# Vision tower on one core: tokenizer with signed differences from PSUM and an earlier start of two units, and unread products in five places

## The chip, the core and the metric

The kernel runs on one core of one Trainium2 chip: a tensor engine (PE, with weight loads shown apart as PEld), a vector engine (DVE), a scalar engine (ACT), GpSimd (POOL), and SyncE (SP), whose queue issues most of the transfers. SBUF is the working memory; matrix products land in PSUM. The metric is the device time of one execution in microseconds, the median of several runs.

## The reference

A batch of 128 images of 128 x 128 goes through a tokenizer, two attention layers and two feed-forward layers, all in float32. The part that this case changes most is the tokenizer: two convolutions, each followed by a batch normalization with given statistics.

```python
def _bn(x, g, b, m, v):
    return (x - m) * (g / jnp.sqrt(v + EPS)) + b
x = _bn(_conv(X, w1, 8), g1, b1, m1, v1)     # 8x8 patches, stride 8, 64 channels: 16 x 16 places
x = _bn(_conv(x, w2, 2), g2, b2, m2, v2)     # 4x4 taps, stride 2, 256 channels: 8 x 8 places
...                                          # rearranged to 64 tokens of 256 per image
h = h + _L0_attn_ref(_layernorm(h), ...)     # relu attention
h = h + _L0_ffn_ref(_layernorm(h), ...)      # a mixture of small attentions
h = h + _L1_attn_ref(_layernorm(h), ...)     # linear attention
h = h + _L1_ffn_ref(_layernorm(h), ...)      # 8 experts, one per token, capacity 1.25
```

The last layer picks one expert for each of the 8192 tokens (argmax of a gate), numbers the tokens within their expert, runs a two-layer network of width 1024 per expert, and adds the result in the order of the tokens.

## The kernel before

One program runs the stages after each other: `tokenizer` (0 to about 174 us of the trace), `relu_attention` (to 1106), `expert_attention` (to 1936), `linear_attention` (to 2276), `route` (to 2325) and `experts` (to 2758). Inside the stages the order of the instructions on every engine is written out by hand (`tc.manual_schedule()`): each engine takes its instructions in the order of the program, and waits where a value or a buffer is not ready.

**Tokenizer.** Partitions hold 64 channels of two halves of the data. The first convolution is done row by row, 16 rows: `conv1(r)` (L123) multiplies the row's 1024 columns by a block-diagonal weight `w1bd` in two matmuls of 512 columns (L130). Each result is a PSUM tile `pa` of a pool with two buffers (`ps1`). The first half, the even places, goes through ACT with scale `s1` and offset `o1` into `ev` (L135, two copies of 64 partitions); the second half, the odd places, goes through DVE into the first third of `h` (L132). `differences(r)` (L139) fills the other two thirds of `h` with even minus odd and odd minus shifted even (L141, L142); `ev` has a column block more than needed, cleared at its edges by six memsets on POOL (L118, L119). `between` (L146) takes differences of whole rows, on POOL (L154) except for two on DVE and one on ACT.

The second convolution is a fast scheme with three products in each direction. For each of 4 row groups `m` and 4 channel blocks `ab` there is a `Unit`: `products(i)` for i = 0, 1, 2 does 12 accumulating matmuls (L177; the trace shows two passes for each) into a PSUM tile `pc` (three buffers); ACT copies one part (`y`, L189), DVE combines the others into `z` (L200, L204); `results(k)` (L210) writes the tokens to `h2`. Combinations of the weight `w` are made on the chip: a sum on POOL (L223), a change of sign on ACT (L226), and `w02`, another sum on POOL (L227).

The order before (L219 to L257): rows 0 to 4 are convolved one after another with their differences; then come the 16 units, and each of the first 11 convolves one more row ahead of its first product (row 5 with unit (0, 0), row 6 with (0, 1), and so on).

**The ends and starts of stages.** `relu_attention` ends with `old.weights()`, `old.transpose()` (PE, L544) and `old.transposed()`, and then the attention products L441. `linear_attention` starts by loading groups, computing their statistics, and transposing on PE, followed by products at L1189. `route` ranks the tokens: scans over one-hot choices, sums over partitions on PE (`pp`, L1685 and L1686), then `past` and `be` (L1736 to L1740: how many blocks lie behind the end of each expert). Then it inverts the permutation by matmuls: for 8 groups of 8 columns, DVE builds one-hot tiles `lh` (L1724) and `hv` (L1727), ACT scales `hv` by the token's number (L1732), and PE accumulates 64 matmuls of 128 x 128 by 78 into `pi` (L1734). `rin` and `rout` from it are the indices for the indirect gathers of `experts` (L1811), whose first block is normalized, transposed (L1842) and multiplied (L1854).

Of the kernel before, what the change touches and what calls it, by code (L numbers as in the profile page):

```python
# [31 lines left out]
class Ctx:  # L32
# [3 lines left out]
    def __init__(self, tc, const):  # L36
# [6 lines left out]
        self.zero = const.tile([P, 8], F32, name="zero")  # L43
        nc.vector.memset(self.zero, 0.0)

    def tables(self, const):


        self.rin = const.tile([P, NTILE], I32, name="rin")
        self.rout = const.tile([P, NTILE], I32, name="rout")  # L50
        self.bexp = const.tile([P, NBLK + 1], I32, name="bexp")
# [10 lines left out]
def tokenizer(c, x, w1, bn1, w2, bn2):  # L62
# [6 lines left out]
    with (  # L69
# [13 lines left out]


        w1bd = wp.tile([P, P], F32, name="w1bd")
        nc.vector.memset(w1bd, 0.0)
        bnv1 = wp.tile([P, 4], F32, name="bnv1")
        bnv2 = wp.tile([P, 4, 4], F32, name="bnv2")
        for k in range(2):
            nc.sync.dma_start(w1bd[k * 64 : (k + 1) * 64, k * 64 : (k + 1) * 64], w1)  # L90
            nc.sync.dma_start(bnv1[k * 64 : (k + 1) * 64, :], bn1)
        load(0, nc.scalar)
        for r in range(1, 3):
            load(r)
# [26 lines left out]
        parts = {}  # L121

        def conv1(r):  # L123

            xt = rows.pop(r)
            parts[r] = h = hp.tile([P, 12, B], F32, tag="h", name="h")
            ev = evens[r % 3]
            for k in range(2):
                pa = ps1.tile([P, 4, B], F32, tag="pa", name="pa")
                nc.tensor.matmul(pa, w1bd, xt[:, 4 * k : 4 * k + 4], start=True, stop=True)  # L130
                if k:
                    nc.vector.tensor_scalar(h[:, 0:4], pa, s1, o1, ALU.mult, ALU.add)  # L132
                else:
                    for o, i in ((ev[0:64, 0:4], slice(0, 64)), (ev[64:128, 1:5], slice(64, P))):
                        nc.scalar.activation(o, pa[i], AF.Identity, bias=o1[i], scale=s1[i])  # L135
            if r + 3 < 16:
                load(r + 3)

        def differences(r):  # L139
            h, ev = parts[r], evens[r % 3]  # L140
# [21 lines left out]
        class Unit:  # L162
# [6 lines left out]
            def products(self, i):  # L169
                m, ab = self.m, self.ab  # L170
                pc = ps2.tile([P, 4, 4, N], F32, tag="pc", name="pc")
                for j, j0 in ((1, 0), (0, 4), (2, 8)):
                    for k in range(2):
                        u = w02[:, k, j] if i == 1 else w[:, k + i, j]
                        for par in range(2):
                            r = slice(par * 64, par * 64 + 64)
                            nc.tensor.matmul(  # L177
                                pc[r, j],
                                u[:, ab * 64 : ab * 64 + 64],
                                part(m, i, k)[:, j0 : j0 + 4, r],  # L180
                                start=(k == 0),
                                stop=(k == 1),
                            )
# [5 lines left out]
                nc.scalar.activation(  # L189
                    y,  # L190
                    pc[:, 1].rearrange("p o n -> p n o"),
                    AF.Identity,
                    bias=o2[:, a] if i == 1 else 0.0,
                    scale=s2[:, a] if i == 1 else 1.0,
                )
                o = self.z[:, i].rearrange("p n (o q) -> p n o q", q=2)
                x = pc[:, 0::2].rearrange("p q o n -> p n o q")
                if i == 1:
                    for q in range(2):
                        nc.vector.scalar_tensor_tensor(  # L200
                            o[:, :, :, q], x[:, :, :, q], s2[:, a], y, ALU.mult, ALU.add
                        )
                else:
                    nc.vector.tensor_add(o, x, bcast(y, 3, 2))  # L204

            def results(self, k):

                ab = self.ab
                f = ab // 2 * 128 + (2 * self.m + k) * 16 + ab % 2 * 8
                nc.vector.scalar_tensor_tensor(  # L210
                    h2[:, :, f : f + 8],
                    self.z[:, 2 * k],
                    (s2, n2)[k][:, ab : ab + 1],
                    self.z[:, 1],
                    ALU.mult,
                    ALU.add,
                )

        with tc.manual_schedule():  # L219
            for r in range(5):  # L220
                conv1(r)
                if r == 1:
                    nc.gpsimd.tensor_add(w[:, :, 1], w[:, :, 0], w[:, :, 2])  # L223
# [36 lines left out]
def relu_attention(c, wqkv, wmlp, bmlp):  # L260
# [8 lines left out]
    with (  # L269
# [387 lines left out]
        with tc.manual_schedule():  # L657
# [426 lines left out]
def linear_attention(c, hd, hx, out, k, wqk, bqk, wv, bv, wgb):  # L1084
# [8 lines left out]
    with (  # L1093
# [543 lines left out]
def route(c, k, gfd):  # L1637
# [5 lines left out]
    with (  # L1643
# [56 lines left out]
        nc.vector.tensor_sub(first, end, nblk)  # L1700
        nc.vector.tensor_scalar_mul(first, first, float(BLK))


        nc.vector.tensor_add(cs, cs, bcast(pp[:, 0], 1, T))
        nc.vector.scalar_tensor_tensor(oh, cs, float(CAP), oh, ALU.is_le, ALU.mult)
# [14 lines left out]
        for t0 in range(0, T, T // NQ):  # L1720
# [11 lines left out]
                nc.scalar.activation(hv[:, i], hv[:, i], AF.Copy, scale=k.token[:, t])  # L1732
            for i in range(T // NQ):
                nc.tensor.matmul(pi, lh[:, i], hv[:, i], start=(t0 + i == 0), stop=(t0 + i == T - 1))  # L1734
            if t0 == 0:
                nc.vector.tensor_tensor(past, bcast(k.blk, 2, E), bcast(end, 1, NBLK), ALU.is_ge)  # L1736
                nc.vector.tensor_reduce(be[:, 0:NBLK], past, AX.X, ALU.add)
                nc.vector.tensor_scalar_min(be[:, 0:NBLK], be[:, 0:NBLK], float(E - 1))
                nc.vector.tensor_copy(be[:, NBLK : NBLK + 1], end[:, E - 1 : E])
                nc.vector.tensor_copy(c.bexp, be)  # L1740
# [9 lines left out]
def experts(c, hx, gfd, out, w1, w2, b2, routing):  # L1750
# [9 lines left out]
    with ExitStack() as nest:  # L1760
# [138 lines left out]
        with tc.manual_schedule():  # L1899
            for n in range(2):  # L1900
                blocks[n].load()
            for n in range(2):
                blocks[n].gather((False,))
            blocks[0].moments()
            blocks[0].normal()
            blocks[0].transpose()
            for n in range(2):
                blocks[n].gather((True,))
            blocks[1].moments()
            blocks[2].gather()  # L1910
            blocks[1].normal()
# [42 lines left out]
def layout(**i):  # L1954
# [9 lines left out]
    o["w1"] = i["L0_tok_w1"].reshape(64, 64)  # L1964
    o["bn1"] = np.stack([i[f"L0_tok_{k}1"] for k in "gbmv"], axis=1)
# [5 lines left out]
    o["bn2"] = bn2.reshape(4, 8, 2, 8, 2).transpose(1, 3, 0, 2, 4).reshape(64, 4, 4)  # L1971
    q, k, v = (i[f"L0_attn_W{n}"].T for n in "qkv")

    v = v.reshape(D, 32, 8).transpose(0, 2, 1).reshape(D, D)
# [45 lines left out]
```

## Time and profile before

| What | Value |
|---|---|
| runs shown | 2759.99, 2768.24, 2768.82 us; median 2768.24 |
| the profiled execution | 2759.7 us; span from the first to the last instruction 2757.9 us |
| mean granted clock of PE | 0.971 |
| busy share | PE 94%, DVE 74%, ACT 59%, POOL 59% |
| first matmul of the first convolution | 7.51 us |
| first matmul of the second convolution | 26.98 us |
| route: `pi` | 2296.84 to 2324.4 us |
| PE idle ahead of the experts' first transpose | 7.9 us |

Busy time is the time in which an engine works on an instruction; the granted clock is 1.00 or 0.50 in the rows of a stretch. A row of a group of instructions gives line, engine, operation, output and inputs, shape and count, then the busy time in all, the mean of one in ns, and the idle time of the engine before them with what ended it.

### The profile page before, as it was taken

What the parts mean: (1) busy time and instruction counts of PE and PEld (TensorE: products, weight loads), DVE (VectorE), ACT (ScalarE), POOL (GpSimd) and SP (SyncE); (2) the same over time, 40 slices, a digit from 0 to 9 for tenths busy, and PEclk for the clock granted to TensorE, in tenths of its full rate; (3) what the DMA queues carried; (4) which work ended last, traced back from release to release, by engine and by line L of the source; (5) the groups of instructions that cost most, each with busy time, mean ns of one, the idle gap of its engine ahead of it and who ended that gap; (6) DMA issues with size and microseconds to landing.
All of it is one profiled execution on the core that took longest, in us unless ns stands there. A gap on an engine that the chain in (4) does not pass through costs nothing. (4 is left out here: it accounts for less than half of the span.)

```text
span 2757.9 us, 76947 instructions
## 1 busy us (share of the span) xinstructions
PE 2602.5 (94%) x33263; PEld 1744.7 (63%) x33263; DVE 2038.5 (74%) x3024; ACT 1628.9 (59%) x3415; POOL 1633.7 (59%) x1390
## 2 busy tenths in 40 slices
PE   8989999999999998899999999999799986999997
PEld 4553444444444443688888888887466565888886
DVE  7769999999998998577778777777367775444443
ACT  3238888888888887466666565665245532233332
POOL 3329888888888887756565656543133312454444
PEclk9999999999999999899999999999899995999998
DMA  3000000000000000000000000000435443555554
GB/s 115 25 13 1 2 1 2 1 2 2 1 2 1 2 2 2 12 11 18 11 18 11 11 18 11 11 19 10 115 64 120 92 116 116 179 198 190 188 196 134
DMA packets 138063, 140.80 MB, mean 51 GB/s; under 512 B 107923, under 2 KB 121509, under 8 KB 130032
## 3 DMA queue, kind: packets, MB, share of 16 engines
q1 hardware_dynamic: 126816, 117.91, 14.3%
q0 software_dynamic: 7648, 14.77, 1.7%
q8 instruction: 263, 4.31, 0.7%
q10 hardware_dynamic: 3248, 3.09, 0.4%
q14 instruction: 88, 0.72, 0.1%
HBM read 103.93 MB, written 32.54 MB: 49 GB/s over the span
## 5 line engine op out<-in xcount | busy, mean ns | idle before, releaser
L495 POOL TENSOR_TENSOR m<-q,k 128x1024 f32<-128x1024 f32 x384 | 719.4, 1905 | 31.2 <-PE sc L297 16.1
L487 DVE TENSOR_TENSOR m<-pc,k 128x2048 f32<-128x2048 f32 (+1 forms) x320 | 646.5, 2057 | 0.5 <-ACT q L431 0.5
L297 PE MATMUL sc<-m,wide 128*32 128x512 f32 x4096 | 529.5, 598 | 12.0 <-DVE m L487 7.2
L496 ACT ACTIVATE m<-m 128x1024 f32<-128x1024 f32 x384 | 402.2, 1049 | 6.0 <-POOL m L495 5.5
L297 PEld LDWEIGHTS sc<-m,wide 128*32 128x32 f32 x4096 | 126.5, 109 | 259.7 <-issue 145.6
L505 ACT ACTIVATE m<-k,q 128x64 f32<-128x64 f32 x1024 | 270.8, 339 | 0.8 <-DVE k L378 0.8
L946 DVE TENSOR_REDUCE mx<-sc 128x16 f32<-128x1024 f32 x128 | 155.9, 1218 | 155.6 <-PE sc L934 125.3
L961 POOL TENSOR_TENSOR e<-e,mx 128x1024 f32<-128x1024 f32 x128 | 243.7, 1904 | 10.1 <-POOL mx L960 0.2
L906 ACT COPY qk<-pqk 128x512 f32<-128x512 f32 x256 | 138.7, 603 | 131.3 <-PE pqk L902 131.3
L960 POOL TENSOR_TENSOR mx<-mx,gate 128x16 f32<-128x16 f32 x128 | 27.8, 217 | 314.2 <-ACT z L991 155.3
L1854 PE MATMUL ph<-xt,w1s 128*128 128x256 f32 x896 | 201.0, 382 | 3.7 <-DVE xt L1845 3.1
L1870 PE MATMUL po<-w2s,hT 128*128 128x256 f32 x896 | 198.0, 379 | 0.0
L973 ACT COPY pT<-pt 128x512 f32<-128x512 f32 x256 | 138.7, 598 | 99.6 <-PE pt L970 98.7
L1854 PEld LDWEIGHTS ph<-xt,w1s 128*128 128x128 f32 x896 | 171.5, 192 | 28.9 <-DVE xt L1845 3.9
L1870 PEld LDWEIGHTS po<-w2s,hT 128*128 128x128 f32 x896 | 168.1, 190 | 21.7
L902 PE MATMUL pqk<-xT,w 64*128 64x128 f32 x2048 | 169.3, 289 | 1.3 <-issue 1.3
L947 DVE TENSOR_TENSOR e<-sc,mx 128x1024 f32<-128x1024 f32 x128 | 156.7, 1224 | 4.4
L1888 POOL DMA_INDIRECT out<-y,rout x56 | 56.8, 1014 | 168.4 <-ACT hT L1858 131.0
L1858 ACT ACTIVATE hT<-ph,w1s 128x256 f32<-128x256 f32 x224 | 93.5, 471 | 103.7 <-PE ph L1854 103.7
L902 PEld LDWEIGHTS pqk<-xT,w 64*128 64x128 f32 x2048 | 142.5, 189 | 18.9 <-issue 10.1
L953 DVE TENSOR_REDUCE mx<-e 128x16 f32<-128x1024 f32 x128 | 153.1, 1196 | 1.3 <-ACT e L950 1.1
L970 PE MATMUL pt<-ident,e 128*128 128x128 f32 x1024 | 143.3, 281 | 4.5 <-issue 0.9
(302 smaller groups left out, 4986.9 us busy)
## 6 DMA issues: line engine op xcount, KB each, us to landing
w1s<-in_we SPq DMA_DIRECT2D x30, 1028.0 KB, 5.2
w2s<-in_we SPq DMA_DIRECT2D x30, 1024.0 KB, 4.9
hd<-h SPq DMA_DIRECT2D x16, 512.0 KB, 3.2
x<-hd SPq DMA_DIRECT2D x16, 512.0 KB, 4.2
h<-hd SPq DMA_DIRECT2D x4, 2048.0 KB, 12.8
hx<-h SPq DMA_DIRECT2D x4, 2048.0 KB, 12.1
out<-h SPq DMA_DIRECT2D x4, 2048.0 KB, 21.3
xt<-in_x SPq DMA_DIRECT2D x15, 512.0 KB, 3.5
```

What stands on the lines that cost most here:

```text
L297: nc.tensor.matmul(dst[j : j + 32], wide[:, hf, s : s + 32], part, start=start, stop=stop)
L487: nc.vector.tensor_tensor(m, bcast(self.pq[:, hf, i : i + n], 3, T), k, ALU.max)
L495: nc.gpsimd.tensor_tensor(m, bcast(self.q[:, hf, s : s + 2], 3, T), k, ALU.subtract)
L496: nc.scalar.activation(m, m, AF.Relu)
L505: nc.scalar.activation(self.parts[i, hf][:, q], self.blk.k[:, hf, i], AF.Relu, bias=self.q[:, hf, i - NB // 2, q : q + 1], scale=-1.0,)
L902: nc.tensor.matmul(pq[par][:, k, eh, :], w[r, f : f + P], self.xT[r, fc], start=True, stop=True)
L946: nc.vector.tensor_reduce(mx, sc, AX.X, ALU.max)
L947: nc.vector.tensor_sub(e, sc, bcast(mx, 2, T))
L953: nc.vector.tensor_reduce(self.sm[x], self.e[x], AX.X, ALU.add)
L961: nc.gpsimd.tensor_mul(e, e, bcast(sm, 2, T))
L1854: nc.tensor.matmul(ph[:, j], self.w1[:, w0 : w0 + P], self.xt[:, fc], start=(fc == 0), stop=(fc == 1))
L1870: nc.tensor.matmul(po, self.hT[:, f, r * P : r * P + P], self.w2[:, f, :], start=(f == 0), stop=(f == 7))
```

## The change

1. `Ctx.busy(out, x, n)` puts n matmuls of the identity by x into a PSUM tile that nobody reads. It is called in five places: ahead of the tokenizer's first row (8 matmuls of 128 columns), ahead of the last transpose of `relu_attention` (5 of 512), at the start of `linear_attention` (3 of 512, once the first group's data is there), in `route` after `past` is known and ahead of `pi` (8 of 312), and in `experts` ahead of the first block's normalization (7 of 512, once the first weights are there).
2. The tokenizer's weight arrives as a block-diagonal 128 x 128 tile in one transfer instead of a memset and two transfers; the two batch normalizations' values arrive in one transfer each, laid out on the host, the second one on SP's queue behind the rows 1 and 2.
3. The odd places are copied with reversed sign (`ns1`, `no1`, made on POOL), the even places without offset; the cleared edges of `ev` are filled with the negative offset instead of zero, by POOL operations on the identity tile. `differences` reads the odd places from their PSUM tile `pa`, which is thus held until then, and subtracts `ev`, by two scalar_tensor_tensor. The signs of the later steps are reversed to match (`n2` and `s2` change places), and the change of sign of a third of `w` on ACT falls away.
4. The order in the tokenizer: rows 0 to 2, then units (0, 0) and (0, 1) are interleaved with rows 3 to 6; from unit (0, 2) and row 7 on the order is as before.
5. In `route` the lines on `past` and `be` stand earlier in the text; the order of DVE's instructions there is unchanged.

```diff
+    def busy(self, out, x, n):
+        for _ in range(n):
+            self.nc.tensor.matmul(out, self.ident, x, start=True, stop=True)
...
-        nc.vector.memset(w1bd, 0.0)
...
-        for k in range(2):
-            nc.sync.dma_start(w1bd[k * 64 : (k + 1) * 64, k * 64 : (k + 1) * 64], w1)
-            nc.sync.dma_start(bnv1[k * 64 : (k + 1) * 64, :], bn1)
+        nc.sync.dma_start(w1bd, w1)
+        nc.sync.dma_start(bnv1, bn1)
...
-        for k in range(2):
-            nc.scalar.dma_start(bnv2[k * 64 : (k + 1) * 64], bn2)
+        nc.sync.dma_start(bnv2, bn2)
...
+        ns1, no1 = (wp.tile([P, 1], F32, name=n) for n in ("ns1", "no1"))
+        nc.gpsimd.tensor_sub(ns1, c.zero[:, 0:1], s1)
+        nc.gpsimd.tensor_sub(no1, c.zero[:, 0:1], o1)
...
-            nc.gpsimd.memset(ev[0:64, 4], 0.0)
-            nc.gpsimd.memset(ev[64:128, 0], 0.0)
+            for r, j in ((slice(0, 64), 4), (slice(64, P), 0)):
+                nc.gpsimd.tensor_scalar(ev[r, j], c.ident[r], c.zero[r, 0:1], no1[r], ALU.mult, ALU.add)
...
-                    nc.vector.tensor_scalar(h[:, 0:4], pa, s1, o1, ALU.mult, ALU.add)
+                    nc.vector.tensor_scalar(h[:, 0:4], pa, ns1, no1, ALU.mult, ALU.add)
+                    odd[r] = pa
...
-                        nc.scalar.activation(o, pa[i], AF.Identity, bias=o1[i], scale=s1[i])
+                        nc.scalar.activation(o, pa[i], AF.Identity, bias=0.0, scale=s1[i])
...
-            nc.vector.tensor_sub(h[:, 4:8], ev[:, 0:4], h[:, 0:4])
-            nc.vector.tensor_sub(h[:, 8:12], h[:, 0:4], ev[:, 1:5])
+            for j in range(2):
+                nc.vector.scalar_tensor_tensor(
+                    h[:, 4 * j + 4 : 4 * j + 8], pa, s1, ev[:, j : j + 4], ALU.mult, ALU.subtract
+                )
...
-            for r in range(5):
-                conv1(r)
-                if r == 1:
-                    nc.gpsimd.tensor_add(w[:, :, 1], w[:, :, 0], w[:, :, 2])
-                differences(r)
-                if r == 1:
-                    nc.scalar.mul(w[:, :, 2], w[:, :, 2], -1.0)
-                    nc.gpsimd.tensor_add(w02, w[:, 0:2], w[:, 2:4])
-                    between(0, 0, 0)
-                elif r == 2:
-                    between(0, 0, 1)
-            for k in range(2):
-                between(0, 2, k)
+            c.busy(ps1.tile([P, P], F32, tag="pa", name="idle"), c.ident, 8)
+            conv1(0)
+            differences(0)
+            conv1(1)
+            nc.gpsimd.tensor_add(w[:, :, 1], w[:, :, 0], w[:, :, 2])
+            nc.gpsimd.tensor_add(w02, w[:, 0:2], w[:, 2:4])
+            differences(1)
+            conv1(2)
+            between(0, 0, 0)
+            differences(2)
+            between(0, 0, 1)
...
+            units = [Unit(0, ab) for ab in range(2)]
+            units[0].products(0)
+            conv1(3)
+            units[0].products(1)
+            differences(3)
+            between(0, 2, 0)
+            units[0].results(0)
+            units[1].products(0)
+            conv1(4)
+            units[1].products(1)
+            differences(4)
+            between(0, 2, 1)
+            units[1].results(0)
+            conv1(5)
+            units[0].products(2)
+            differences(5)
+            units[0].results(1)
+            between(1, 0, 0)
+            conv1(6)
+            units[1].products(2)
+            differences(6)
+            units[1].results(1)
             for m in range(4):
-                for ab in range(4):
+                for ab in range(0 if m else 2, 4):
...
             old.weights()
+            c.busy(psq.tile([P, 8, T], F32, tag="pq", name="idle"), blocks[-1].k[:, 0, 0:8], 5)
             old.transpose()
...
                 groups[g].load()
+            c.busy(psp.tile([P, 2, D], F32, tag="pp", name="idle"), groups[0].x[:, 0:2], 3)
...
+        idle = gpp.tile([P, NBLK, E], F32, name="idle")
+        c.busy(idle, past, 8)
...
+            c.busy(psh.tile([P, 2, BLK], F32, tag="ph", name="idle"), blocks[0].w1[:, 0:512], 7)
             blocks[0].moments()
```

More of the change, by code (lines that the diff above doesn't have):

```diff
@@ L114, in tokenizer @@
         s1, o1 = scale_offset(lambda i: bnv1[:, i : i + 1], [P, 1], "1")
+        ns1, no1 = (wp.tile([P, 1], F32, name=n) for n in ("ns1", "no1"))
+        nc.gpsimd.tensor_sub(ns1, c.zero[:, 0:1], s1)
+        nc.gpsimd.tensor_sub(no1, c.zero[:, 0:1], o1)
         evens = [wp.tile([P, 5, B], F32, name=f"ev{k}") for k in range(3)]
         for ev in evens:
-            nc.gpsimd.memset(ev[0:64, 4], 0.0)
-            nc.gpsimd.memset(ev[64:128, 0], 0.0)
-        parts = {}
+            for r, j in ((slice(0, 64), 4), (slice(64, P), 0)):
+                nc.gpsimd.tensor_scalar(ev[r, j], c.ident[r], c.zero[r, 0:1], no1[r], ALU.mult, ALU.add)
+        parts, odd = {}, {}
         def conv1(r):
@@ L139, in differences @@
         def differences(r):
-            h, ev = parts[r], evens[r % 3]
-            nc.vector.tensor_sub(h[:, 4:8], ev[:, 0:4], h[:, 0:4])
-            nc.vector.tensor_sub(h[:, 8:12], h[:, 0:4], ev[:, 1:5])
+            h, ev, pa = parts[r], evens[r % 3], odd.pop(r)
+            for j in range(2):
+                nc.vector.scalar_tensor_tensor(
+                    h[:, 4 * j + 4 : 4 * j + 8], pa, s1, ev[:, j : j + 4], ALU.mult, ALU.subtract
+                )
         taken = {}
@@ L193, in products @@
                     bias=o2[:, a] if i == 1 else 0.0,
-                    scale=s2[:, a] if i == 1 else 1.0,
+                    scale=n2[:, a] if i == 1 else 1.0,
                 )
@@ L200, in products @@
                         nc.vector.scalar_tensor_tensor(
-                            o[:, :, :, q], x[:, :, :, q], s2[:, a], y, ALU.mult, ALU.add
+                            o[:, :, :, q], x[:, :, :, q], n2[:, a], y, ALU.mult, ALU.add
                         )
@@ L212, in results @@
                     self.z[:, 2 * k],
-                    (s2, n2)[k][:, ab : ab + 1],
+                    (n2, s2)[k][:, ab : ab + 1],
                     self.z[:, 1],
@@ L1701, in route @@
         nc.vector.tensor_scalar_mul(first, first, float(BLK))
+        nc.vector.tensor_tensor(past, bcast(k.blk, 2, E), bcast(end, 1, NBLK), ALU.is_ge)
+        nc.vector.tensor_reduce(be[:, 0:NBLK], past, AX.X, ALU.add)
+        nc.vector.tensor_scalar_min(be[:, 0:NBLK], be[:, 0:NBLK], float(E - 1))
+        nc.vector.tensor_copy(be[:, NBLK : NBLK + 1], end[:, E - 1 : E])
+        nc.vector.tensor_copy(c.bexp, be)
+        idle = gpp.tile([P, NBLK, E], F32, name="idle")
+        c.busy(idle, past, 8)
         nc.vector.tensor_add(cs, cs, bcast(pp[:, 0], 1, T))
@@ L1734, in route @@
                 nc.tensor.matmul(pi, lh[:, i], hv[:, i], start=(t0 + i == 0), stop=(t0 + i == T - 1))
[L1735 to L1740, printed above, removed]
         id1 = gp.tile([P, NTILE], F32, name="id1")
@@ L1963, in layout @@
     o["x"] = np.concatenate(x, axis=1)
-    o["w1"] = i["L0_tok_w1"].reshape(64, 64)
-    o["bn1"] = np.stack([i[f"L0_tok_{k}1"] for k in "gbmv"], axis=1)
+    o["w1"] = np.zeros((P, P), np.float32)
+    for k in range(2):
+        o["w1"][k * 64 : k * 64 + 64, k * 64 : k * 64 + 64] = i["L0_tok_w1"].reshape(64, 64)
+    o["bn1"] = np.tile(np.stack([i[f"L0_tok_{k}1"] for k in "gbmv"], axis=1), (2, 1))
     w2 = i["L0_tok_w2"].reshape(4, 4, 64, 8, 2, 8, 2).transpose(0, 1, 2, 4, 6, 3, 5).reshape(4, 4, 64, D)
@@ L1969, in layout @@
     bn2 = np.stack([i[f"L0_tok_{k}2"] for k in "gbmv"], axis=0)
-    o["bn2"] = bn2.reshape(4, 8, 2, 8, 2).transpose(1, 3, 0, 2, 4).reshape(64, 4, 4)
+    o["bn2"] = np.tile(bn2.reshape(4, 8, 2, 8, 2).transpose(1, 3, 0, 2, 4).reshape(64, 4, 4), (2, 1, 1))
     q, k, v = (i[f"L0_attn_W{n}"].T for n in "qkv")
```

## The prediction

> **What bounds the kernel now.** I read the totals, then the stretches around each touched place, then single instructions there. TensorE is busy nearly throughout:
>
> ```profile
> PE 2602.5 (94%) x33263; PEld 1744.7 (63%) x33263; DVE 2038.5 (74%) x3024; ACT 1628.9 (59%) x3415; POOL 1633.7 (59%) x1390
> ```
>
> So what counts is where PE waits, or works at half clock. The table by stretches (columns: length, busy PE, PEld, DVE, ACT, POOL, granted clock, DMA) shows both:
>
> ```profile
> 21.18:24.59 3.41, 1.74 (x4) 0.68 (x5) 3.31 (x4) 1.55 (x2) 0.00 (x0) 1.00 0.48 154
> 171.37:174.78 3.41, 0.80 (x8) 0.27 (x4) 2.56 (x6) 0.38 (x1) 0.20 (x1) 1.00 0.00 0
> 1092.97:1096.38 3.41, 0.48 (x16) 0.49 (x18) 0.93 (x3) 0.63 (x1) 1.04 (x1) 1.00 0.01 2
> 2270.57:2273.98 3.41, 0.33 (x1) 0.00 (x0) 3.14 (x11) 0.00 (x0) 0.00 (x0) 1.00 0.88 218
> 2273.98:2277.39 3.41, 0.42 (x2) 0.46 (x3) 3.13 (x11) 0.00 (x0) 0.00 (x0) 0.50 0.82 208
> 2297.87:2301.28 3.41, 3.41 (x18) 3.41 (x18) 1.08 (x2) 2.67 (x11) 0.00 (x0) 0.50 0.95 363
> 1946.30:1949.71 3.41, 0.00 (x0) 0.00 (x0) 2.92 (x12) 0.00 (x0) 0.65 (x2) 0.50 1.08 372
> 1953.12:1956.54 3.42, 3.42 (x8) 2.06 (x9) 0.41 (x2) 2.68 (x6) 1.67 (x4) 0.50 0.26 47
> 2335.42:2338.83 3.41, 3.41 (x9) 2.69 (x9) 0.74 (x2) 0.78 (x2) 2.79 (x5) 0.50 0.02 0
> ```
>
> The clock changes only on a grid of 3.41 us. It fell after the second, third and fourth stretch (PE busy 0.33 to 0.80 us) and stayed after the first (1.74 us). PE was busy for all of 2297.87:2301.28 at half clock and the clock did not rise: those matmuls stream only 78 columns. This is the route stage, until 2324.47:
>
> ```profile
> L1734 PE MATMUL pi<-hv,lh 128*128 128x78 f32 x128 | 27.6, 422 | 8.1 <-ACT hv L1732 8.1
> L1732 ACT ACTIVATE hv<-hv,token 128x78 f32<-128x78 f32 x64 | 16.8, 346 | 21.2 <-DVE hv L1727 21.2
> L1724 DVE TENSOR_TENSOR lh<-lo,at 128x1024 f32<-128x1024 f32 x8 | 9.8, 1224 | 9.7 <-PE pi L1734 9.7
> L1727 DVE TENSOR_TENSOR hv<-lo,at 128x624 f32<-128x624 f32 x8 | 6.4, 800 | 0.0
> ```
>
> DVE waits 9.7 us for PE here, so PE's clock sets this stage. The tokenizer's timeline gives the prices of its start:
>
> ```profile
> 7.51 3.65 PE L130 MATMUL pa<-xt,w1bd 128*128 128x512 f32 x4 [7.51 <-DMA w1bd<-in_w]
> 9.98 2.34 POOL L223 TENSOR_TENSOR w<-w 128x1024 f32<-128x1024 f32 x1
> 10.62 1.57 ACT L135 ACTIVATE ev<-pa,o,s 64x512 f32<-64x512 f32 x2
> 11.21 0.81 DVE L132 TENSOR_SCALAR h<-pa,s,o 128x512 f32<-128x512 f32 x1 [1.97 <-PE pa L130]
> 12.07 1.98 PE L130 MATMUL pa<-xt,w1bd 128*128 128x512 f32 x4 [0.90 <-DVE h L132]
> 26.98 2.81 PE L177 MATMUL pc<-v,w 128*64 128x256 f32 x24
> ```
>
> Rows 0 to 4 come first, held by evacuations; from 26.98 PE has no gap until 172.2. The first row's passes took 3.65 us, a later row's 1.98: PE started cold although the clock column says 1.00.
>
> **The sum's base.** Prices come from the profiled execution: 2759.7 us, a span of 2757.9 and 1.8 around it. It is the lowest of the runs shown (2759.99, 2768.24, 2768.82; median 2768.24), 8.5 under the median. No trace shows what the longer ones lose. An estimate: were the clock to rise only with the dense products, rows 1 to 4 would each take 3.65 instead of 1.98 us, 6.7 us in all.
>
> **Tokenizer.** *Prologue.* POOL's order in the changed program is: power of s1, the w add (2.34), ns1, no1, six pad fills, the w02 add (3.66). The add waits for both halves of w; the first odd row waits for ns1, thus for the add. With w there by about 9: 9 + 2.34 + 2 x 0.25 = 11.9, against 11.21. The fills are POOL tensor_scalars of 64x128: 128x4 costs 0.25 and 128x256 1.22 elsewhere in this trace, so 0.3 to 0.72 each instead of 0.20 for the memset; I take 0.7, being nearer in size to the second.
>
> *First product.* The odd PSUM tile is now held until the differences have read it (before: until its 0.81 us copy). From the odd copy at 11.9: copy 0.81, two differences at 0.8 each, pass pair 0.99, and again for rows 1 and 2: 11.9 + 3 x 2.4 + 2 x 0.99 = 21.1; then the DVE difference for the unit's second operand, 1.76: 22.9. The first product starts a little before and is held at its third matmul, which is like starting at 22.6, 4.4 us earlier than 26.98.
>
> *PE's work from there.* A unit without a row takes 7.77 us, with one 9.83: a row costs about 1.9 as PE work. Before, 11 rows lie behind the first product: 26.98 + 16 x 7.77 + 11 x 1.9 = 172.2, which is the end measured. After, 13 rows do: 22.6 + 124.3 + 24.7 = 171.6. So the reordering alone wins only 0.6.
>
> *New waits on PE.* There are two conv buffers. In the built program the second half of rows 5, 6 and 7 waits for that row's own even copies (ACT, 1.57), since the other buffer is still held by the row before. Each loses about 1.57 + 0.3 of hand-over: 3 x 1.9 = 5.7 (bounds 2 and 7). Behind the waiting half stand the products, since PE goes in order. Row 4's second and row 7's first half wait for DVE differences queued behind the units' combinations (0.4 to 0.9 each): 0 to 3, I take 1.5. Unit 0's last product needs the difference between(0,2,1), queued on DVE behind the combinations: about 8 us of DVE work (0.81 + 0.69 + 0.9 + 1.6 + 1.76 + results at 0.75, more when POOL holds it up; L210's mean is 1.82) against 6.4 of PE: 1 to 4, I take 2.5. A late w, the fills ahead of w02, and a cold stretch between the sparse rows: 0 to 5, I take 2.3. In steady state the longer hold costs nothing, because rows 8 to 15 lie 9.8 us apart; the differences' freedom from POOL's long subtraction (L141 took 2.83 instead of 0.69 beside it) gains nothing while PE bounds, and the bias, sign and load edits hide beside it. The sum is -0.6 + 5.7 + 1.5 + 2.5 + 2.3 = **+11.4** (bounds +2 and +18).
>
> The 8 idle products at the start (16 passes, 3.4 us cold) run before the first input lands and cost nothing; they serve the slow first row and make later runs alike.
>
> **Route.** 8 products of 312 columns are 16 passes x 0.52 = 8.3 us cold, from about 2291 (when `past` is there) in place of idleness until 2296.84. They fill one whole grid step, so the clock rises at 2294.46 or 2297.87, and they can hold `pi` by 0 to 1 us, I take 0.5. At full clock a pass of `pi` takes 0.107 instead of 0.2145 (27.6/128): 16 passes are 1.7 us a group. DVE's 1.22 + 0.80 and ACT's 8 x 0.26 bound a group at 2.1: 2296.9 + 8 x 2.1 + 0.3 = 2314 instead of 2324.4, **-10** with the hold (bounds -3 and -10.5). The transfers of the first weights end near 2314, so the gathers do not run into them. Does it stay warm? A 512-column pass takes 0.43 us at full clock, 78 columns stream 0.065: 16 x 0.065 / 2.2 = 0.47 of the time. The stretch 21.18:24.59 streamed 3.2 passes, 0.40, and stayed warm; by the same count no step in the trace after which the clock fell streamed more than about 0.36.
>
> [...]
>
> **The other three.** Experts: 14 passes x 0.43 = 6.0 us inside PE's idle 2324.47 to 2332.29, covered by gather and normalization. The transposes then take 0.60 instead of 1.09, and the 4.64 us of cold L1854 half: **-2.8** if the clock is warm at their start; cold, 12 us would overrun that wait and cost up to +3. Linear attention: 6 passes x 0.853 = 5.1 from 1946.5; the rise comes at 1949.71 instead of 1956.54, and the 3.42 busy in 1953.12:1956.54 halves: **-1.7** (0 to -2). End of relu attention: 10 passes x 0.43 = 4.3 fit into the wait 1091.26 to 1095.89; the cold 3.4 us behind go, **-0.9** (0 to -1.7).
>
> Sum: 2759.7 + 11.4 - 10 - 2.8 - 1.7 - 0.9 = 2755.7, taken as 2756, 0.44% under the median. The bound of 0.3%, about what a measurement of this kernel can tell, is 8.3 us: faster means under 2759.9, slower over 2776.5.
>
> **Rivals.** (1) *Slower: the held buffer also stalls rows 8 to 15.* If the second half of every row waits for its own even copies, eight more stalls of 1.9 add 15 us, and with the tokenizer's other terms at their upper ends (+6.6): 2755.7 + 15 + 6.6 = 2777. It decides by who frees the second half's buffer in the steady units: in the built program a DVE count that is old by then, which speaks against it. (2) *The route cools down again* after one or two steps: -3 instead of -10, thus 2763; if the experts' products then start cold, +3 instead of -2.8, 2769. For it: 0.47 is close to 0.36. (3) *The tokenizer breaks even*, its waits hidden as the two early units leave DVE slack: 2755.7 - 9 = 2747. For it: 4.4 us of earlier start. (4) *The idle products do not lift the clock* and only the tokenizer's loss is left: 2771; against it, PE's dense products lift it within a step elsewhere.
>
> **How the numbers follow.** Forecast 0.46, rival 1 0.15, rival 2 0.20, rival 3 0.13, rival 4 0.06. Faster: rival 3 and all of the forecast but 0.03 at its upper edge, 0.56. Slower: 0.10 of rival 1 (its price lies at the bound) and 0.03 of rival 2 (2769 with the tokenizer's +6.6), 0.13. Same: the rest, 0.31. The forecast alone covers 2749 to 2762. The range, 2744 to 2772, takes in rivals 2, 3 and 4; outside are rival 1, the end of rival 2 and a little at the bottom.
>
> **What would show it.** Right: `pi` at full clock over some 17 us; 1.00 in the experts' first step; the tokenizer's last product near 183; rows 5 to 7 with gaps of about 1.9 us put down to the even copies. Wrong: a last product at 172 or 190; half clock back inside `pi`; transposes of the experts held behind idle products.

## The result, and the profile after

| | before | after |
|---|---|---|
| median of 20 runs | 2763.49 us (2757.43 to 2771.78) | 2761.72 us (2756.29 to 2766.92) |
| ratio | | 0.9992, 95% interval 0.9983 to 1.0 |
| profiled execution | 2759.7 us, span 2757.9 | 2762.18 us, span 2760.1 |
| mean granted clock | 0.971 | 0.979 |

The change made no difference of more than 0.3%: 1.8 us less, inside the predicted range, but not the 12 us that were forecast. Before's 20 runs fall into groups, nine at 2757 to 2761 us, eight at 2768 to 2772 and three between; its profiled execution lies in the lower group, so the two profiled executions differ by +2.5 us where the medians differ by -1.8. The single parts moved much more than the sum. The same instructions can be looked up in both traces; how much later they come after the change is a ledger:

| Mark | before | after | later by | step |
|---|---|---|---|---|
| last product of the tokenizer starts | 171.8 | 185.3 | 13.5 | +13.5 |
| last attention product of `relu_attention` | 1103.5 | 1116.4 | 12.9 | -0.6 |
| last output product of `expert_attention` | 1935.0 | 1948.9 | 13.9 | +1.0 |
| first product of `linear_attention` | 1954.2 | 1970.4 | 16.2 | +2.3 |
| first matmul of `pi` | 2296.8 | 2310.6 | 13.8 | -2.4 |
| last matmul of `pi` | 2324.0 | 2328.5 | 4.5 | -9.3 |
| first hidden product of the experts | 2334.2 | 2338.1 | 3.9 | -0.6 |
| last product of the experts | 2739.1 | 2741.4 | 2.3 | -1.6 |

The route's 9 us pay for two thirds of what the tokenizer loses. Steps of about 1 us in this ledger can be chance: in e8 below, which has before's code up to the route, the last output product of `expert_attention` came 1.5 us later than before's (1936.5 against 1935.0). PE's total after:

```profile
PE 2616.1 (95%) x33325; PEld 1744.2 (63%) x33325; DVE 2030.1 (74%) x3023; ACT 1624.8 (59%) x3414; POOL 1636.9 (59%) x1392
```

The tokenizer's timeline after (start, duration, engine, line, operation; in brackets the idle time before it and what ended it; L136 is a row's convolution, L138 the odd copy, L142 the even copies, L149 the differences, L163 a difference of whole rows, L186 a unit's product):

```profile
8.79 1.12 PE L136 MATMUL pa<-xt,w1bd 128*128 128x512 f32 x2 [0.78 <-ACT ev L142]
10.59 2.33 POOL L233 TENSOR_TENSOR w<-w 128x1024 f32<-128x1024 f32 x1 [4.81 <-DMA w<-in_w]
13.26 0.81 DVE L138 TENSOR_SCALAR h<-pa,ns,no 128x512 f32<-128x512 f32 x1 [6.90 <-POOL no L119]
15.82 3.78 PE L136 MATMUL pa<-xt,w1bd 128*128 128x512 f32 x4 [5.90 <-DVE h L149]
27.15 3.99 PE L186 MATMUL pc<-v,w 128*64 128x256 f32 x20 [2.96 <-DVE v L163]
43.00 1.12 PE L136 MATMUL pa<-xt,w1bd 128*128 128x512 f32 x2
45.60 1.12 PE L136 MATMUL pa<-xt,w1bd 128*128 128x512 f32 x2 [1.47 <-ACT ev L142]
```

Row 0's odd half lay in PSUM by 8 us, but DVE waited 6.90 us for `no1`, which stands behind the w add on POOL, and that waited 4.81 us for w. PE stood 5.90 us, its clock fell (0.50 from 14.1 to 24.4), and the next four passes took 3.78 us. The first unit's product got through at 27.15, no earlier than before's 26.98. The last two lines are row 5: its second half waits 1.47 us for the row's own even copies. Rows 6 and 7 (52.71 and 59.10) show the same.

The route after, as a group of instructions, and the stretches from there into the experts (length, busy PE, PEld, DVE, ACT, POOL, granted clock, DMA):

```profile
L1774 PE MATMUL pi<-hv,lh 128*128 128x78 f32 x128 | 16.8, 289 | 1.4 <-ACT hv L1772 1.4
```

```profile
2318.10:2321.50 3.40, 2.92 (x24) 2.77 (x24) 3.21 (x4) 2.83 (x13) 0.00 (x0) 1.00 1.01 422
2335.17:2338.58 3.41, 1.58 (x7) 0.82 (x7) 1.90 (x6) 0.00 (x0) 2.83 (x4) 1.00 0.15 41
2338.58:2342.00 3.42, 3.42 (x10) 2.71 (x9) 0.54 (x3) 0.39 (x2) 2.69 (x5) 0.50 0.02 0
```

`pi` now keeps the full clock to its end, in 17.9 us instead of 27.2. But the experts' idle products end at 2335.5, the transposes start at 2336.6, and in this step PE works only 1.58 us: the clock falls, and the first hidden products run at half clock for one step.

At the start of `linear_attention` the idle products did harm:

```profile
1962.23 4.95 PE L49 MATMUL idle<-x,ident 128*128 128x512 f32 x6 [1.44 <-DMA x<-hd]
1967.26 2.07 ACT L1183 ACTIVATE x<-x,nb,rs 128x256 f32<-128x256 f32 x4 [19.60 <-PE idle L49]
```

ACT normalizes `x` in place, the idle products read the same `x`, and so ACT waits for PE, 0.8 us after its factors were ready (nb at 1966.45). By the last of the products that start here (2209.3 before, 2223.4 after) the lag is 14.1 us, about that ahead of the stage (13.9).

### The profile page after: what moved, and what is told of

Its sections match the earlier page's. It is cut to its first block, busy times and chain, and to the rows that moved or that the text cites. A ratio compares the mean times of both kernels' runs of the same rounds, so it can differ in the third digit from the quotient of the medians.

```text
span 2760.1 us, 77058 instructions
## 1 busy us (share of the span) xinstructions
PE 2616.1 (95%) x33325; PEld 1744.2 (63%) x33325; DVE 2030.1 (74%) x3023; ACT 1624.8 (59%) x3414; POOL 1636.9 (59%) x1392
## 5 line engine op out<-in xcount | busy, mean ns | idle before, releaser
L1888 PEld LDWEIGHTS ph<-xt,w1s 128*128 128x128 f32 x896 | 171.0, 191 | 27.6 <-DVE xt L1879 2.2
```

What stands on the lines that cost most here:

```text
L1888: nc.tensor.matmul(ph[:, j], self.w1[:, w0 : w0 + P], self.xt[:, fc], start=(fc == 0), stop=(fc == 1))
```

## The experiments

All are compared with the kernel before on the same chip, with 6 to 12 runs of each.

**e1_idle_only**: the unread products without the tokenizer's edits.

```diff
+            c.busy(ps1.tile([P, P], F32, tag="pa", name="idle"), c.ident, 8)
             for r in range(5):
                 conv1(r)
...
+            c.busy(...)   # the other four places as in the change
```

> The kernel before with only the five groups of unread products (and the lines on past and be moved up). Theory: the change holds two halves of opposite sign, the unread products win about 11 us (route -9.4, end of relu attention -0.9, experts -1 to -2, linear attention about 0) and the tokenizer loses 13.5. Then this kernel has its tokenizer's last product near 171 and takes about 2748 us, 0.994 of before; and since its first rows are warm, its runs spread less than before's (under 6 us). Rival: what the route wins is given back behind it, by the later clock or the gathers; then it stays within 0.3% of before, 2757 or more.

Measured: 2752.02 us against 2764.55, ratio 0.9953 (0.9939 to 0.9968). So the unread products win 12 us and the tokenizer's edits give most of it away again. The runs did not come together, though: three lie at 2748.7 to 2749.1, as expected, and three at 2755.0 to 2757.9. The profiled one is of the upper group, and its rows show why. Timeline of e1 (L135 is a row's convolution, L147 the second difference of a row, L233 POOL's sum `w02`):

```profile
7.48 3.75 PE L135 MATMUL pa<-xt,w1bd 128*128 128x512 f32 x4 [2.15 <-DMA w1bd<-in_w]
12.14 6.19 PE L135 MATMUL pa<-xt,w1bd 128*128 128x512 f32 x8 [0.90 <-DVE h L137]
16.97 3.90 POOL L233 TENSOR_TENSOR w<-w 128x1536 f32<-128x1536 f32 x1 [4.82 <-ACT w L232]
17.51 3.91 DVE L147 TENSOR_TENSOR h<-h,ev 128x512 f32<-128x512 f32 x1
22.20 1.13 PE L135 MATMUL pa<-xt,w1bd 128*128 128x512 f32 x2 [3.87 <-DVE h L137]
24.59 3.78 PE L135 MATMUL pa<-xt,w1bd 128*128 128x512 f32 x4 [1.27 <-ACT ev L140]
```

The idle products end at 5.3, PE waits 2.15 us for the input, and behind row 0 part of rows 1 and 2 still runs at half clock (6.19 us for the two, against 1.98 each in e8 below). That is the smaller part of the loss. It delays row 1's second difference on DVE by 1.8 us against e8, but POOL's sum `w02` by only 0.9, so that the difference now starts behind the sum instead of ahead of it: it takes 3.91 us instead of 0.68, PE waits 3.87 us for DVE ahead of row 3, the granted clock falls to 0.50 from 23.7 to 33.9, and the rest of row 3 and row 4 are slow too (24.59 is the second half of row 3 and the first of row 4). The last product starts at 179.5, that of e8 at 171.9.

**e2_tok_only**: the changed kernel without its five `c.busy` calls.

```diff
-            c.busy(...)   # all five
```

> The changed kernel without any unread products: the tokenizer's edits alone. Theory: the tokenizer's last product is at 185 or later (the start is cold too), pi takes 27.6 us as before, and the time is 2773 to 2778 us, about 1.004 to 1.005 of before. Rival: the tokenizer's loss is only that before's profiled run was a lucky one; then it is within 3 us of before's median, 2761 to 2766.

Measured: 2769.73 us against 2764.55, ratio 1.0024 (1.0013 to 1.0036); last product at 183.8, `pi` 27.2 us. The tokenizer's edits alone cost 5 us: slower, as the theory has it, but by less than it said. Before's runs on this chip spread from 2756 to 2769 us, and its profiled run is of the faster ones; that the longer ones end their tokenizer near 179.5 like e1 is likely, but no trace of before shows it. The rival is half right on this point. The changed kernel's last product is later by 1.5 us than e2's (185.3 against 183.8), so the idle products ahead of the first row won nothing in these two traces.

**e3_pool_first**: `ns1`, `no1` and the fills ahead of the w add on POOL.

```diff
         with tc.manual_schedule():
+            nc.gpsimd.tensor_sub(ns1, c.zero[:, 0:1], s1)
+            nc.gpsimd.tensor_sub(no1, c.zero[:, 0:1], o1)
+            ...   # the six fills, moved in here: their order is then the written one
             conv1(0)
```

> The changed kernel with POOL's order turned: ns1, no1 and the six fills stand ahead of the w add, which waits for w (10.59 us in the profile after). Theory: the first odd copy starts near 8 instead of 13.26, rows 1 and 2 follow, and the first unit's products get through some 4 to 6 us earlier; the waits at rows 4 to 6 for their own even copies stay. Last product near 180, time about 2757 us, 0.998 of the kernel after. Rival: the rows are held by the PSUM tiles and the w02 add anyway, so that the products come at most 1.5 us earlier and the time stays at 2760 to 2762.

Measured: 2753.82 us, ratio 0.9961 (0.9948 to 0.9975), thus 0.3% less than the changed kernel. The products get through at 20.51 instead of 27.15, the last one starts at 178.7 instead of 185.3: 6.6 us earlier at both ends. POOL's order was half of the tokenizer's loss.

**e4_old_order**: the changed kernel with before's order of rows and units.

```diff
-            conv1(0); differences(0); conv1(1); ...   # rows 0 to 2, then two units among rows 3 to 6
+            for r in range(5):
+                conv1(r)
+                ...
-                for ab in range(0 if m else 2, 4):
+                for ab in range(4):
```

> The changed kernel (differences from PSUM, unread products) with the order of before: rows 0 to 4 first, then each unit with one row. Theory: the waits for a row's own even copies vanish from the units, since the rows lie 9.8 us apart, but all five rows are now held at the start by the PSUM tiles, first products at 32 to 36; the last product near 178 to 181, time 2754 to 2758 us. Rival: the held PSUM tile alone makes the loss, in any order: last product at 185 or later, 2762 us or more. Second rival: the order alone makes it, and the start is no later than before's 27: last product 172, 2749 us.

Measured: 2755.23 us, ratio 0.9967 (0.9955 to 0.9979); first products at 34.6, last at 179.4. As expected, the waits for a row's own even copies are gone from the units, and the first products come 7.6 us later than before's; 5.8 us of that is PE's wait behind `ns1` and the w add, as in the changed kernel. Neither rival holds: the last product is neither at 185 nor at 172.

**e5_warm_rows**: e1 with 18 idle products ahead of the first row and 4 behind each of the rows 0 to 4.

```diff
-            c.busy(ps1.tile([P, P], F32, tag="pa", name="idle"), c.ident, 8)
+            idle = ps2.tile([P, 4, 4, N], F32, tag="pc", name="idle")
+            c.busy(idle[:, 0, 0:2], c.ident, 18)
             for r in range(5):
                 conv1(r)
+                c.busy(idle[:, 0, 0:2], c.ident, 4)
```

> e1_idle_only with 18 instead of 8 idle products of 128 columns ahead of the first row and 4 behind each of the rows 0 to 4, into a PSUM tile of the units. Theory: before's tokenizer ends at 172 or at 179.5, as the rows 0 to 4 meet the full or the half clock (in e1 the idle products end at 5.3, PE then waits 2.2 us for the first input, and the clock falls again); if the rows are kept warm, the last product is at 172 or earlier in every run, the runs lie within 5 us of each other, and the median is 2748 to 2750 us, 0.9945 of before. Rival: the half clock of the rows has no part in it (their evacuations bound them); then two groups of runs remain, 8 us apart, and the median is 2752 or more, with the added products costing up to 3 us.

Measured: 2750.05 us against 2761.02, ratio 0.9953 (0.9936 to 0.9969). The runs lie between 2746.6 and 2753.6 without a gap (7.0 us, not the expected 5), the upper group at 2755 to 2758 is gone, and in the profiled run the last product starts at 174.4: between the theory's 172 and e1's 179.5. PE waited once for 2.9 us in row 3 and lost the clock for one step. Warm rows did not prevent this wait, because it is e1's: row 1's second difference, started at 14.93 behind POOL's sum at 14.83, took 3.92 us. The intervals of e1 and e5 overlap; that warmth alone is worth 2 us in the median is likely, not shown.

**e6_sbuf_diff**: e3 with the differences from the copy in SBUF.

```diff
...   # the offset back in the even copies, zeros at the edges
-                    h[:, 4 * j + 4 : 4 * j + 8], pa, s1, ev[:, j : j + 4], ALU.mult, ALU.subtract
+                    h[:, 4 * j + 4 : 4 * j + 8], h[:, 0:4], -1.0, ev[:, j : j + 4], ALU.mult, ALU.subtract
```

> e3_pool_first with the differences taken from the copy in SBUF (minus h minus ev, two operations), the offset back in the even copies and zeros at their edges; so the odd PSUM tile is free after its copy. The new order of rows and units stays. Theory: the held tile makes the three waits for a row's own even copies (1.47 us of idle, 1.9 with the hand-over, at rows 4, 5 and 6); they go, and the last product comes 4 to 6 us earlier than e3's 179, time 2748 to 2750 us. Rival: the two buffers alternate in such a way that the waits belong to the order and not to the hold; then the last product stays at 178 to 180 and the time at 2753 to 2755 us.

Measured: 2754.55 us, ratio 0.9964 (0.9952 to 0.9976), last product at 178.8: the same as e3. The waits for the even copies are gone, so they do belong to the held tile; the rival is wrong on that, and right on the time, for a reason that neither had. Timeline of e6:

```profile
10.82 2.35 POOL L230 TENSOR_TENSOR w<-w 128x1024 f32<-128x1024 f32 x1 [2.69 <-DMA w<-in_w]
11.71 5.82 DVE L141 SCALAR_TENSOR_TENSOR h<-h,ev 128x512 f32<-128x512 f32 x2
13.24 3.74 POOL L231 TENSOR_TENSOR w<-w 128x1536 f32<-128x1536 f32 x1
```

and of e3, where the same differences read PSUM:

```profile
12.89 3.43 POOL L232 TENSOR_TENSOR w<-w 128x1536 f32<-128x1536 f32 x1
12.96 1.40 DVE L142 SCALAR_TENSOR_TENSOR h<-pa,s,ev 128x512 f32<-128x512 f32 x2
```

With both inputs in SBUF, row 1's two differences took 5.82 us and ended only after POOL's second sum; with one input in PSUM they took 1.40 us beside the same sum. By what DVE and POOL hold each other up here, no run shows.

**e8_route_only**: the kernel before with the route's idle products alone.

```diff
...   # the lines on `past` and `be` stand earlier, as in the change
+        idle = gpp.tile([P, NBLK, E], F32, name="idle")
+        c.busy(idle, past, 8)
```

> The kernel before with the route's idle products alone. Theory: pi at full clock to its end, 18 instead of 27.6 us, 9 us less than before, 0.9967, with before's two groups of runs 8 us apart still there. Rival: the route's gain is lost in part behind it, since the experts' first step starts cold after a shorter route and the gathers meet the weight transfers: 5 us or less, 0.998 or more.

Measured: 2756.68 us against 2761.02, ratio 0.9981 (0.997 to 0.9992). `pi` took 17.8 us, as in every kernel with these products. The profiled run took 2751.73 us, 8.0 less than before's profiled one; both have their last tokenizer product at 171.8 to 171.9. The medians differ by only 4.3 us, which is the rival's size; the interval, 2 to 8 us, leaves out the theory's 9. But the rival's reason is not what the traces show, since nothing is lost behind the route: the last matmul of `pi` comes 8.2 us earlier than before's (2315.8 against 2324.0) and so does the last product of the experts (2730.9 against 2739.1). What makes the difference of the medians smaller stays open. Timeline of e8, with row 1 at full clock and DVE ahead of POOL's sum, where e1 had the half clock and DVE behind it:

```profile
12.17 1.98 PE L135 MATMUL pa<-xt,w1bd 128*128 128x512 f32 x4 [0.91 <-DVE h L137]
15.74 0.68 DVE L147 TENSOR_TENSOR h<-h,ev 128x512 f32<-128x512 f32 x1
16.05 3.66 POOL L232 TENSOR_TENSOR w<-w 128x1536 f32<-128x1536 f32 x1 [3.79 <-ACT w L231]
```

**e7_mended**: e5 with idle products in `linear_attention` that read the weight, and longer ones in the experts.

```diff
-            c.busy(psp.tile(...), groups[0].x[:, 0:2], 3)
+            c.busy(psp.tile(...), w[:, 0].rearrange("p (a d) -> p a d", a=2), 5)
...
-            c.busy(psh.tile(...), blocks[0].w1[:, 0:512], 7)
+            c.busy(idle, blocks[0].w1[:, 0:512], 8)
             ...
             blocks[0].transpose()
+            c.busy(idle, blocks[0].w1[:, 0:512], 1)
```

> e5_warm_rows with two of the idle groups changed: in linear attention 5 products from the weight w, which nobody overwrites, instead of 3 from the tile that ACT normalizes in place; in the experts 8 instead of 7, and one more behind the first transposes. Theory: the normalization no longer waits for PE (0.8 us in the profile after), the first products of linear attention and of the experts run at full clock instead of losing it again at 1969.9 and 2338.6 (3.4 us each at half clock): 3 to 4 us less than e5_warm_rows. Rival: the start of linear attention is set by the transfers and the experts' by the gathers, so that less than 1.5 us is won, or the longer groups overrun their waits and it is up to 2 us slower.

Measured: 2746.06 us, ratio 0.9937 (0.9918 to 0.9955), 4 us less than e5, though the two intervals overlap and the profiled runs differ by 2.0 us. In `linear_attention` ACT starts 4.4 us behind the first statistics, as before the change (5.1 after it), and the clock is full from 1953.7 on, ahead of the first products at 1956.8. The experts' first step stays at full clock (stretches of e7):

```profile
2317.40:2320.80 3.40, 3.25 (x11) 1.34 (x10) 1.48 (x5) 0.00 (x0) 2.79 (x4) 1.00 0.27 81
2320.80:2324.20 3.40, 3.40 (x15) 2.39 (x14) 1.70 (x5) 0.34 (x1) 2.48 (x4) 1.00 0.01 0
```

From the last matmul of `pi` to the first output product it is 17.0 us, against 18.7 in e5 and 19.9 in the kernel before.

**e9_hybrid**: e3 with PSUM differences for rows 0 to 2 only, SBUF differences from row 3.

```diff
-                    odd[r] = pa
+                    odd[r] = pa if r < 3 else None
...   # from row 3 the even copies with offset, zero edges and two more buffers
+                x, f = (h[:, 0:4], -1.0) if pa is None else (pa, s1)
                 nc.vector.scalar_tensor_tensor(
-                    h[:, 4 * j + 4 : 4 * j + 8], pa, s1, ev[:, j : j + 4], ALU.mult, ALU.subtract
+                    h[:, 4 * j + 4 : 4 * j + 8], x, f, ev[:, j : j + 4], ALU.mult, ALU.subtract
```

> e3_pool_first with two ways of taking the differences: rows 0 to 2 from the held PSUM tile as in the change, rows 3 to 15 from the SBUF copy as in e6 (even copies with offset and zero edges, in two more buffers). Theory: the two ways each lose once. SBUF differences of the first rows wait while POOL sums w (in e6 those of row 1 took 5.8 instead of 1.3 us beside L230 and L231); held tiles make PE wait for the own row's even copies at rows 4 to 6 (e3, 3 x 1.5 us). The hybrid has neither: the first unit's products as early as e3's (third matmul near 20.5), no wait for an even copy behind row 3, last product 4 to 6 us ahead of e3's 178.7, time 2748 to 2750 us. Rival: the order itself costs the time, through DVE (the difference for unit 0's last product, 2 us late in e6): last product at 177 or later, 2752 us or more.

(The rows meant are 5 to 7, not 4 to 6.) Measured: 2749.78 us, ratio 0.995 (0.9935 to 0.9966); products through at 19.29, last one at 175.7, 3.0 us ahead of e3's. Each way of taking the differences loses in one place, and the hybrid avoids both. The step is smaller than the 4 to 6 us expected: unit 0's last product now waits 2.1 us for its DVE difference (0.5 in e3), a wait that the row waits had covered, and its 20 passes behind it took 4.07 us instead of 2.38.

**e10_hybrid_warm**: e9 with e7's groups and idle products among the first rows.

```diff
...   # the groups of e7 in `linear_attention` and the experts; `idle` as in e5
-            c.busy(ps1.tile([P, P], F32, tag="pa", name="idle"), c.ident, 8)
+            c.busy(idle, c.ident, 9)
...
             conv1(0)
+            c.busy(idle, c.ident, 4)
...
             conv1(1)
+            c.busy(idle, c.ident, 6)
...
             conv1(2)
+            c.busy(idle, c.ident, 12)
```

> e9_hybrid with the mended idle groups of e7_mended and idle products between rows 0 to 2 and the first unit (9, 4, 6 and 12 of 128 columns). Theory: 3.5 us from the mended groups (e7 against e5 was 4.0) and 1 to 3 us from a full clock over the first unit, which ran at half clock in e3 and e6: 2743 to 2746 us, at or under e7's 2746. Rival: the idle products stand in the way of the rows and units as much as they quicken them: 2747 or more, and e7 with the old tokenizer stays the best.

Measured: 2744.36 us against 2765.57, ratio 0.9933 (0.9915 to 0.995): the fastest, though not told apart from e7. PE's waits in the first 70 us (total, times, longest), of the kernel after and then of e10:

```profile
PE pa L136 <- ACT ev L142: 6.7, 5, 1.5
PE pa L136 <- DVE h L149: 5.9, 1, 5.9
PE pc L186 <- DVE v L163: 3.5, 2, 3.0
```

```profile
PE pc L180 <- DVE v L157: 2.9, 2, 2.1
...
PE pa L129 <- ACT ev L135: 0.5, 1, 0.5
PE pa L129 <- DVE h L143: 0.4, 1, 0.4
```

16.1 us of waits became 3.8, and the last product starts at 171.8: with all that, the new order only draws level with before's best start.

## Why the prediction was right and wrong

**The base.** The forecast stood 12 us under a median of three runs, 2768.24. The median of 20 is 2763.49: before's runs spread over more than the three showed, and 4.7 us of the forecast gain were in the base. The estimate of 6.7 us for cold rows 1 to 4 is near the 7.6 us that two traces with before's tokenizer differ by, 171.9 (e8) and 179.5 (e1), but partly by luck: 3.2 us of e1's chain are a DVE difference behind POOL's sum, which the estimate did not have.

**Tokenizer, +11.4 predicted, +13.5 measured.** The size is nearly right by luck: its terms are wrong in both directions. (a) The step "11 rows lie behind the first product" is a miscount: six rows are convolved by 26.98, so ten lie behind it and thirteen after the change. Taking a row at 9.83 - 7.77 = 2.06, before is 26.98 + 16 x 7.77 + 10 x 2.06 = 171.9, and the three rows moved behind the first product cost 6.2 us, not 3.8. (b) The early start was worth nothing. The step "w there by about 9" failed: it came at 10.59, the odd copy at 13.26 instead of 11.9, and the waiting PE went cold (clock 0.50 from 14.1 to 24.4), so that the unit got through at 27.15 and not at 22.6. The mechanism, POOL's order, was the right one, as e3 shows. (c) The waits for the own even copies came at rows 5, 6 and 7 as said, 1.47 us each instead of 1.9. (d) Row 4's and 7's other waits, 1.5 by the prediction, did not appear; unit 0's last product waited 0.50 instead of 2.5. (e) The differences' freedom from POOL was taken to gain nothing because PE bounds; in the first rows PE waits for them, and there it counts: row 1's took 1.40 us in e3 and 5.82 in e6. (f) The eight idle products did not make the runs alike: the 20 runs after the change spread over 10.6 us, the 11 of e2 without them over 7.3.

**Route, -10 predicted, -9.3 measured.** Right in the mechanism: the clock rose during the idle products (at 2307.9) and stayed. A group takes 2.34 us instead of 2.1: a pass takes 0.131 us (16.8/128) instead of 0.107, so two groups are 4.2 us of PE work, and they come every 4.68 us, with 0.48 us of waiting for ACT. (27.6/128 is 0.216 and not 0.2145, which changes nothing.) At 24 passes in a step of 3.40 us this streams 24 x 0.065 = 1.57 us, 0.46 of the time, as estimated. No profiled kernel with these products lost the clock inside `pi` (median of a matmul's duration 275 to 288 ns in all ten, 421 before), so rival 2 did not come.

**Experts, -2.8 predicted, -0.6 at the first product and -2.2 by the end.** The transposes still met the full clock, but the step that failed is the halving of "the 4.64 us of cold L1854": 14 passes end 1 us before the transposes, the step of the grid that holds the transposes has 1.58 us of work, and the first hidden products come at half clock behind it. One product more and one behind the transposes mended it (e7).

**Linear attention, -1.7 predicted, +2.3 measured.** The dependency was overlooked: the idle products read a tile that ACT overwrites. The other 1.5 us are the first load: its statistics start 13.2 us behind the last output product, against 11.6 in before. In the ten experiments' traces this is 11.4 to 12.1 us, whether they have idle products here or not, so it does not belong to the change. The clock rose at 1966.5, fell again at 1969.9 behind the sparse transposes (PE busy for 2.18 of 3.41 us), and so did not help the first products. Ahead of `pi` the 2.3 us had come back (the ledger's -2.4); what brought them back was not tested.

**End of relu attention, -0.9 predicted, -0.6 measured.** Right in the clock, which stays at 1.00 up to 1123.3 where before's stood at 0.50 in 1096.38:1099.79; a step of 0.6 us alone would prove nothing.

**The rivals.** Rival 1's stalls in rows 8 to 15 did not come: rows from 8 on take 1.98 us without a wait. Rival 4 is excluded by `pi`, rival 3 by the last product at 185.3. The time fell between the forecast and rival 2, in the case "same" that had 0.31, not in "faster" with 0.56. In the traces the last product comes 2.3 us later where the terms sum to 4.0 us earlier: the start of linear attention makes 4.0 of the 6.3 us between them, though most of it came back, the tokenizer 2.1.

## What to carry to other kernels

An idle product has to read something that nobody waits to overwrite (ACT waited 0.8 us for one in `linear_attention`), has to bridge the whole gap up to the real work and into it (the experts lost the clock behind a step with 1.58 us of work), and paid most here ahead of work that did not raise the clock by itself but kept it (`pi`, 27.2 us without the products and 17.9 with them). With one input in PSUM, row 1's differences took 1.40 us beside POOL's sum (e3), with both in SBUF 5.82 (e6); in exchange the held PSUM buffer made PE wait 1.47 us a row, at rows 5 to 7: choose it where GpSimd is busy, not where the buffers are short. Where both inputs are in SBUF, look which of the two engines starts first (0.68 us for a difference ahead of POOL's sum in e8, 3.91 behind it in e1). Before a median of three is taken as a base, look whether the runs fall into groups, and take the profiled run's group for the sum.

## What the hardware showed unexpectedly

A delay of 1.8 us, behind rows at half clock, decided in e1 which of two other engines went first. In e8 row 1's second difference started 0.31 us ahead of POOL's sum and took 0.68 us; in e1 it started 0.54 us behind it and took 3.91. With the wait and the fallen clock that followed, the last product of the tokenizer lies 7.6 us apart (171.9 and 179.5). Why the rows met the full clock in one and not in the other fits the 3.41 us grid (the 25 changes of the clock in before's trace lie whole multiples of 3.41 us apart): before's row 0 fills a whole step (PE busy for all of 7.53:10.94), and row 1 ran at full clock; counted back from the fall at 23.7, e1's steps begin at 6.6 and 10.0, and its row 0, from 7.48 to 11.2, fills none. No run moved the start against the grid to test this.

PE busy all the time did not raise the clock (27.6 us of `pi` at 0.50 before). Nor did the busy share alone tell whether it stayed: `pi` kept it with PE busy for 2.92 of 3.40 us, and before kept it behind 21.18:24.59 with 1.74 of 3.41, but it lost it behind 2198.89:2202.30 with 2.53.
